# Merging the weighted sums of two graphs into one run of 128 tiled matmuls, with a separate PSUM pool for the scores and an earlier attention window

## Chip, cores, metric

One core of one Trainium2 chip. The metric is the device time of one execution in microseconds (us). "The trace" is the profiler's record of one execution.

## The reference, cut to what matters

Two layers on 128 graphs of 128 nodes with 256 features, all in fp32. Layer 0 applies graph attention twice and a feed-forward part. Layer 1 is an eight-head attention in which each of four relations has its own value projection:

```python
scores = jnp.einsum('bhid,bhjd->bhij', q, k) / np.sqrt(dh)
attn = jax.nn.softmax(scores, axis=-1)
for r in range(Wv.shape[0]):                     # 4 relations
    v_r = (src @ Wv[r] + bv[r]).reshape(Bb, Nn, h, dh).transpose(0, 2, 1, 3)
    mask = (adj_matrix == r)[:, None]
    out = out + jnp.einsum('bhij,bhjd->bhid', attn * mask, v_r)
attn_out = out.transpose(0, 2, 1, 3).reshape(Bb, Nn, Dm) @ Wo + bo
x = _ln(src + attn_out, g1, beta1)
ff = jax.nn.gelu(x @ W1 + b1, approximate=False) @ W2 + b2
return _ln(x + ff, g2, beta2)
```

## The kernel before

The 128 graphs go through in 32 groups of four (G = 4). Each stage of a group is a Python generator. A stage has a **window**, a begin and an end in units of one group, and the stages of all groups are interleaved by that clock; a scheduler then fixes the order on each engine. The parts that matter here:

```python
TB, KB = 4, 7                                    # buffers of T and of tok
ps = ctx.enter_context(tc.tile_pool(name="ps", bufs=5, space=PSUM))
# 8 PSUM banks in use: "mm" 5, "tr" 2 (transposes), "av" 1 (weighted sums)

def weights(b):                                  # scores and softmax of graph b
    scores = [ps.tile([P, DC, 2, N], F32, name="mm") for _ in range(2)]
    for c in range(DC):
        for h in range(2):                       # two halves of the array's rows
            rows = ts(h, P // 2)
            nc.tensor.matmul(scores[h][:, c], qT[rows, c, ts(b, N)], kbd[c][rows, b],
                             start=True, stop=True, tile_position=(h * P // 2, 0))
    ...                                          # maximum, 4 exponentials a bank, division

def weighted(ms, v):                             # 32 calls, 64 instructions
    po = ps.tile([P, DC, N], F32, name="av", bufs=1)
    for c in range(DC):
        for r in reversed(range(R)):
            for q in reversed(range(HC)):        # 4 column tiles of 32
                last = nc.tensor.matmul(po[ts(q, DH), c], v[:, r, ...], ms[q // 2][r][:, ...],
                                        start=r == R - 1, stop=r == 0, tile_position=(0, q * DH))
    ...

for b in range(G):
    ...
    ms = by_relation(b, es.pop(0))               # 8 masked tiles on VectorE
    v = values(b)
    yield 1.5
    with tc.high_priority(offset=200):
        oT, last = weighted(ms, v)
        if b + 2 < G:
            with tc.issue_after(last.ins):       # on TensorE's queue: not ahead of this run
                es.append(weights(b + 2))
    ...

stages = (..., (stage_attention, 16, 2.0, 3.0), ...)   # steps, begin, end
```

Every fp32 matmul call shows as two instructions in the trace (transposes as one), so one graph's scores are a block of 8 and its weighted sum is a run of 64.

## Time and profile before

| | before |
|---|---|
| median (3 runs) | 3509.6 us |
| profiled span | 3506.2 us |
| TensorE busy | 98% |
| steady period of one group | 107.33 us |
| span minus 32 periods ("start and end") | 71.6 us |

In profile lines, PE is TensorE's matmuls, PEld its weight loads, DVE VectorE, ACT ScalarE, POOL GpSimd; L352 is line 352 of the kernel. In a timeline line, the first number is the start, the second the modelled length of the merged group of instructions. I take the time of a group from the start of the next one. The period is the distance between the first query projections (L286) of two groups.

### The profile page before, as it was taken

To read this page: it belongs to the slowest core of one execution; us is meant where nothing else is said; L and a number is where in the kernel's file an instruction comes from. 1 tells how busy PE (TensorE), PEld (TensorE's weight loads), DVE (VectorE), ACT (ScalarE), POOL (GpSimd) and SP (SyncE) were. 2 spreads that over 40 slices of the span, in tenths; PEclk is the share of its full clock that TensorE was granted. 3 is DMA by queue.
4 is the path that set the end of the run, shared out by engine and by line. 5 is a ranking of instruction groups with operands and counts; after the bars stand their busy time and mean duration, and the time that the engine had idled before them with its cause. 6 is when DMAs were issued, how large, how long until landed. Compare 5 with 4: busy or idle time off the path is not lost.

```text
span 3506.2 us, 52290 instructions
## 1 busy us (share of the span) xinstructions
PE 3442.3 (98%) x20496; PEld 2256.7 (64%) x20496; DVE 1602.0 (46%) x3529; ACT 1692.8 (48%) x4702; POOL 1167.7 (33%) x1352
## 2 busy tenths in 40 slices
PE   7999999999999999999999999999999999999998
PEld 5566666666666666666666666666666666666655
DVE  2444445444445444454344554444544445544453
ACT  3455445555445554455554455544555444555342
POOL 2223323233233233332332332433323323324332
PEclk8999999999999999999999999999999999999999
DMA  4000000000000000000000000000000000000000
GB/s 179 7 10 22 22 22 16 7 22 22 22 16 13 16 22 22 22 16 7 22 22 22 16 7 22 22 22 22 16 7 22 22 22 10 7 10 7 7 7 13
DMA packets 23925, 70.87 MB, mean 20 GB/s; under 512 B 2432, under 2 KB 6016, under 8 KB 23552
## 3 DMA queue, kind: packets, MB, share of 16 engines
q1 hardware_dynamic: 23680, 67.53, 5.5%
q8 instruction: 162, 2.65, 0.3%
q14 instruction: 83, 0.68, 0.1%
HBM read 50.75 MB, written 16.78 MB: 19 GB/s over the span
## 4 chain that ended last, share of the span: by engine, by line
PE 85%; ACT 9%; DVE 5%; issue 1%; POOL 0%; DMA 0%; SPq 0%; ACTq 0%; POOLq 0%; DVEq 0%
PE mm L210 25%; PE mm L222 20%; PE mm L340 12%; PE av L352 7%; ACT kbd L295 5%; PE mm L255 3%; PE mm L286 3%; PE mm L379 3%; PE tr L327 3%; PE mm L304 2%; PE mm L273 2%; PE mm L292 2%; PE mm L264 2%; ACT e L242 2%; PE tr L193 1%; ACT tr L235 1%
## 5 line engine op out<-in xcount | busy, mean ns | idle before, releaser
L331 DVE SCALAR_TENSOR_TENSOR m<-at,tr 128x512 f32<-128x512 int32 x1024 | 628.3, 679 | 229.3 <-PE av L352 134.5
L184 POOL TENSOR_TENSOR tok<-tok,ln_rows 128x512 f32<-128x512 f32 x508 | 634.8, 1274 | 280.0 <-PE tr L193 260.8
L316 POOL TENSOR_TENSOR e<-e,s 128x512 f32<-128x512 f32 x256 | 264.0, 1041 | 759.1 <-DVE mv L170 666.2
L213 ACT ACTIVATE fT<-mm,col 128x512 f32<-128x512 f32 x512 | 337.9, 687 | 331.4 <-PE mm L210 327.4
L210 PE MATMUL mm<-T,wf 128*128 128x512 f32 x1024 | 473.7, 601 | 11.7 <-ACT T L197 11.7
L210 PE MATMUL mm<-T,w 128*128 128x512 f32 x1024 | 476.4, 604 | 3.6 <-ACT T L197 0.7
L340 PE MATMUL mm<-wv,T 128*128 128x512 f32 x1024 | 461.0, 592 | 0.6 <-ACT e L314 0.6
L222 PE MATMUL mm<-w,fT 128*128 128x256 f32 x2048 | 460.3, 381 | 0.0
L222 PE MATMUL mm<-wf,fT 128*128 128x256 f32 x2048 | 456.0, 381 | 0.0
L178 ACT ACTIVATE tok<-tok,nmr,rstd 128x256 f32<-128x256 f32 x512 | 265.8, 590 | 389.1 <-POOL nmr L176 389.1
L222 PEld LDWEIGHTS mm<-w,fT 128*128 128x128 f32 x2048 | 384.2, 190 | 69.7 <-issue 21.5
L223 DVE TENSOR_TENSOR tok<-tok,mm 128x512 f32<-128x512 f32 x128 | 88.0, 687 | 733.5 <-PE mm L222 730.5
L222 PEld LDWEIGHTS mm<-wf,fT 128*128 128x128 f32 x2048 | 384.3, 190 | 57.1 <-issue 7.4
L314 ACT ACTIVATE e<-mm,nm 128x128 f32<-128x128 f32 x1024 | 357.9, 385 | 17.1 <-DVE nm L310 16.7
L210 PEld LDWEIGHTS mm<-T,w 128*128 128x128 f32 x1024 | 182.9, 190 | 221.0 <-issue 184.9
L210 PEld LDWEIGHTS mm<-T,wf 128*128 128x128 f32 x1024 | 185.9, 191 | 212.9 <-issue 186.6
L340 PEld LDWEIGHTS mm<-wv,T 128*128 128x128 f32 x1024 | 189.5, 190 | 203.3 <-issue 197.1
L244 POOL TENSOR_TENSOR e<-e,s 128x512 f32<-128x512 f32 x64 | 66.5, 1039 | 737.1 <-DVE s L243 737.1
L352 PEld LDWEIGHTS av<-m,v 128*32 128x32 f32 x8192 | 217.3, 110 | 69.8 <-issue 59.6
L352 PE MATMUL av<-m,v 128*32 128x128 f32 x8192 | 252.0, 275 | 7.4 <-DVE v L341 4.7
L356 ACT COPY oT<-av 128x256 f32<-128x256 f32 x128 | 46.9, 366 | 394.0 <-PE av L352 394.0
L314 ACT ACTIVATION_READ_ACCUMULATOR e<-mm,nm 128x1 f32 x1024 | 231.9, 226 | 0.0
(64 smaller groups left out, 3735.6 us busy)
## 6 DMA issues: line engine op xcount, KB each, us to landing
xt<-in_xT_dram SPq DMA_DIRECT2D x32, 512.0 KB, 3.3
tok<-in_x_dram SPq DMA_DIRECT2D x32, 512.0 KB, 3.5
out_dram<-tok SPq DMA_DIRECT2D x31, 512.0 KB, 2.6
at<-in_adjT_dram SPq DMA_DIRECT2D x32, 256.0 KB, 2.7
wf<-in_wf_dram SPq DMA_DIRECT2D x2, 1024.0 KB, 10.9
w<-in_w_dram SPq DMA_DIRECT2D x2, 1024.0 KB, 12.8
ln_rows<-in_rows_dram SPq DMA_DIRECT2D x1, 1024.0 KB, 9.8
wv<-in_wv_dram SPq DMA_DIRECT2D x1, 1024.0 KB, 10.4
```

The lines of the kernel that those rows point to most:

```text
L178: nc.scalar.activation(y[:, b], y[:, b], AF.Identity, bias=nmr[:, b:b + 1], scale=rstd[:, b:b + 1])
L184: engine.tensor_tensor(y[:, b:b + 2], y[:, b:b + 2], v[:, None, :].to_broadcast([P, 2, D]), op)
L210: nc.tensor.matmul(p, win[:, c, ts(f0 + i, P)], hT[:, c], start=c == 0, stop=c == DC - 1)
L213: nc.scalar.activation(t, p, func, bias=bin_[:, f0 + i:f0 + i + 1])
L222: nc.tensor.matmul(p[:, b - b2_], fT[f][:, ts(b, N)], wout[:, f], start=f == 0, stop=f == FC - 1)
L255: nc.tensor.matmul(p, xt[:, c, ts(b, N)], wx[:, c], start=c == 0, stop=c == DC - 1)
L295: nc.scalar.activation(kbd[c][rows, :, q % 2], p[rows], AF.Identity, bias=bk[rows, c:c + 1])
L314: nc.scalar.activation(e[:, q], p[:, q], AF.Exp, bias=nm[:, q:q + 1], accum_out=s[:, q:q + 1])
L316: nc.gpsimd.tensor_mul(e, e, per_row(s, N))
L331: nc.vector.scalar_tensor_tensor(m, ab, r, pT, op0=OP.is_equal, op1=OP.mult)
L340: nc.tensor.matmul(p, hT[:, f, ts(b, N)], wv[:, f, r:r + 2], start=f == 0, stop=f == DC - 1)
L352: last = nc.tensor.matmul(po[ts(q, DH), c], v[:, r, c * P + q * DH:c * P + (q + 1) * DH], ms[q // 2][r][:, c * 2 + q % 2], start=r == R - ...
```

## The change

The intent is to visit the 32-column shape of the array half as often, and to have the next scores follow the run directly, from banks of their own. Sixteen masked tiles need space, which smaller pools and an earlier, longer attention window give back.

```diff
-    TB, KB = 4, 7
+    TB, KB = 3, 6
-    ps = ctx.enter_context(tc.tile_pool(name="ps", bufs=5, space=PSUM))
+    ps = ctx.enter_context(tc.tile_pool(name="ps", bufs=3, space=PSUM))
     ... (fT: FC + 1 to FC buffers; cap, wh, oT: 2 to 1)
-            scores = [ps.tile([P, DC, 2, N], F32, name="mm") for _ in range(2)]
+            scores = [ps.tile([P, DC, 2, N], F32, name="sc", bufs=2) for _ in range(2)]
-                    m = wk.tile([P, HC, N], F32, name="m", bufs=DC * R)
+                    m = wk.tile([P, HC, N], F32, name="m", bufs=2 * DC * R)
-        def weighted(ms, v):
-            po = ps.tile([P, DC, N], F32, name="av", bufs=1)
+        def weighted(work):
+            po = ps.tile([P, 2, DC, N], F32, name="av", bufs=1)
+            for i, (ms, v) in reversed(list(enumerate(work))):
     ... (the same 32 matmuls for each of two graphs, one copy out)
-        for b in range(G):
+        for b0 in range(0, G, 2):
     ... (masks and values of b0 and b0 + 1)
+            with tc.high_priority(offset=200):
+                oT, last = weighted(work)
+                if b0 + 2 < G:
+                    with tc.issue_after(last.ins):
+                        es.append(weights(b0 + 2))
+            yield 1.5
     ... (output projection and addition for both graphs)
+            if b0 + 2 < G:
+                es.append(weights(b0 + 3))
+            yield 1.5
-              (stage_attention, 16, 2.0, 3.0), (stage_ff1, 8.5, 3.15, 3.65))
+              (stage_attention, 16, 1.5, 2.8), (stage_ff1, 8.5, 3.15, 3.65))
```

More of the change, by code (lines that the diff above doesn't have):

```diff
@@ L99, in graph_layers @@
     MW = D + 4
-    m = wload("M", wk.tile([P, DC, MW], F32, name="m_in", tag="wh"))
-    w2T = wload("W2T", wk.tile([P, DC, D], F32, name="w2T", tag="fT", bufs=FC + 1))
+    m = wload("M", wk.tile([P, DC, MW], F32, name="m_in", tag="wh", bufs=1))
+    w2T = wload("W2T", wk.tile([P, DC, D], F32, name="w2T", tag="fT", bufs=FC))
     first_xt = ld.tile([P, DC, T], F32, name="xt")
     nc.sync.dma_start(first_xt, xT[0])
-    w1T = wload("W1T", wk.tile([P, DC, D], F32, name="w1T", tag="fT", bufs=FC + 1))
+    w1T = wload("W1T", wk.tile([P, DC, D], F32, name="w1T", tag="fT", bufs=FC))
     first_at = ld.tile([P, G, N], I32, name="at", bufs=4)
@@ L211, in feed_forward @@
             for i, p in enumerate(pair):
-                t = wk.tile([P, T], F32, name="fT", tag="fT", bufs=FC + 1)
+                t = wk.tile([P, T], F32, name="fT", tag="fT", bufs=FC)
                 nc.scalar.activation(t, p, func, bias=bin_[:, f0 + i:f0 + i + 1])
@@ L247, in gat_block @@
     def gat_block(xg, xt, at):
-        cap = wk.tile([P, G, N], F32, name="cap")
+        cap = wk.tile([P, G, N], F32, name="cap", bufs=1)
         nc.vector.tensor_scalar(cap, at, 0, 2 * BIG, op0=OP.is_gt, op1=OP.mult)
-        wh = wk.tile([P, G, MW], F32, name="wh", tag="wh")
+        wh = wk.tile([P, G, MW], F32, name="wh", tag="wh", bufs=1)
         for b in range(G):
@@ L343, in values @@
             return v
-        def weighted(ms, v):
-            po = ps.tile([P, DC, N], F32, name="av", bufs=1)
-            for c in range(DC):
-                for r in reversed(range(R)):
-                    for q in reversed(range(HC)):
-                        last = nc.tensor.matmul(po[ts(q, DH), c], v[:, r, c * P + q * DH:c * P + (q + 1) * DH],
-                                                ms[q // 2][r][:, c * 2 + q % 2],
-                                                start=r == R - 1, stop=r == 0, tile_position=(0, q * DH))
-            oT = wk.tile([P, DC, N], F32, name="oT")
+        def weighted(work):
+            po = ps.tile([P, 2, DC, N], F32, name="av", bufs=1)
+            for i, (ms, v) in reversed(list(enumerate(work))):
+                for c in range(DC):
+                    for r in reversed(range(R)):
+                        for q in reversed(range(HC)):
+                            last = nc.tensor.matmul(po[ts(q, DH), i, c],
+                                                    v[:, r, c * P + q * DH:c * P + (q + 1) * DH],
+                                                    ms[q // 2][r][:, c * 2 + q % 2],
+                                                    start=r == R - 1, stop=r == 0, tile_position=(0, q * DH))
+            oT = wk.tile([P, 2, DC, N], F32, name="oT", bufs=1)
             nc.scalar.copy(oT, po)
@@ L363, in attention @@
         yield 1
-        for b in range(G):
-            if b % 2 == 0:
-                affine(y, "02", b)
-            ms = by_relation(b, es.pop(0))
-            v = values(b)
-            yield 1.5
-            with tc.high_priority(offset=200):
-                oT, last = weighted(ms, v)
-                if b + 2 < G:
-                    with tc.issue_after(last.ins):
-                        es.append(weights(b + 2))
+        for b0 in range(0, G, 2):
+            affine(y, "02", b0)
+            work = []
+            for b in (b0, b0 + 1):
+                ms = by_relation(b, es.pop(0))
+                work.append((ms, values(b)))
+                yield 1.5
[4 more added lines that the diff above has]
+                        es.append(weights(b0 + 2))
+            yield 1.5
+            p = ps.tile([P, 2, D], F32, name="mm")
+            for i in range(2):
+                for k in range(DC):
+                    nc.tensor.matmul(p[:, i], oT[:, i, k], wo[:, k], start=k == 0, stop=k == DC - 1)
+            nc.vector.tensor_add(y[:, b0:b0 + 2], y[:, b0:b0 + 2], p)
+            if b0 + 2 < G:
+                es.append(weights(b0 + 3))
             yield 1.5
-            p = ps.tile([P, D], F32, name="mm")
-            for k in range(DC):
-                nc.tensor.matmul(p, oT[:, k], wo[:, k], start=k == 0, stop=k == DC - 1)
-            nc.vector.tensor_add(y[:, b], y[:, b], p)
         normalised(y)
```

## The prediction

> **What bounds the kernel now.** I read the first part of the page (busy time by engine), then the chain that ended last, then two steady stretches of the trace by engine, and at last the timeline of TensorE's matmuls, start by start. The first part of the page, with the chain's shares by engine below it:
>
> ```profile
> PE 3442.3 (98%) x20496; PEld 2256.7 (64%) x20496; DVE 1602.0 (46%) x3529; ACT 1692.8 (48%) x4702; POOL 1167.7 (33%) x1352
> ...
> PE 85%; ACT 9%; DVE 5%; issue 1%; POOL 0%; DMA 0%; SPq 0%; ACTq 0%; POOLq 0%; DVEq 0%
> ```
>
> TensorE (PE) is busy 98% of the span, no other engine reaches half, and the chain is 85% PE. So only what shortens or holds up PE's queue counts. Next, busy time by engine in two adjacent stretches of 107.3 us in the middle (columns: stretch, its us, then each engine's busy us and instructions):
>
> ```profile
> 1840.00:1947.30 107.30, 106.81 (x641) 70.02 (x641) 49.87 (x111) 52.95 (x148) 36.51 (x42) 1.00 0.05 18
> 1947.30:2054.60 107.30, 106.81 (x641) 70.02 (x641) 49.87 (x111) 52.94 (x148) 36.51 (x42) 1.00 0.05 18
> ```
>
> The program repeats itself to the hundredth: 107.3 us for each of the 32 groups of four graphs, or 3434 us; the remaining 72 us are start and end. PE idles 0.5 us of each period, at full clock (1.00). But busy is not streaming. In the timeline (start, modelled length, engine, line) I use the distance between starts, because the lengths overlap:
>
> ```profile
> 1852.04 5.34 PE L222 MATMUL mm<-w,fT 128*128 128x256 f32 x24
> 1857.31 1.95 PE L352 MATMUL av<-m,v 128*32 128x128 f32 x64
> 1859.19 1.99 PE L222 MATMUL mm<-w,fT 128*128 128x256 f32 x8
> 1861.03 1.46 PE L273 MATMUL mm<-wh,e 128*128 128x256 f32 x6
> 1862.41 1.14 PE L304 MATMUL mm<-kbd,T 64*128 64x256 f32 x8
> 1863.48 0.70 PE L273 MATMUL mm<-wh,e 128*128 128x256 f32 x2
> ...
> 1864.78 7.07 PE L222 MATMUL mm<-w,fT 128*128 128x256 f32 x32
> 1871.69 1.03 PE L379 MATMUL mm<-wo,oT 128*128 128x256 f32 x4
> ```
>
> The undisturbed L222 costs (1871.69 - 1864.78)/32 = 0.216 us each. The 24 ahead of the weighted sum (L352, 32-column tiles) take 5.27 us instead of 5.18, so **entering** costs 0.09 to 0.10. The 64 small matmuls take 1.88 us; single starts in the trace come in fours 0.110 us apart, so 64 need 1.76, and **leaving** costs about 0.13. The 8 L222 behind it take 1.84 instead of 1.73: another 0.11 **after leaving**. One visit to the 32-column shape therefore costs about 0.10 + 0.13 + 0.11 = **0.34 us** beyond its work, and none of it shows as idle. Over all starts in the trace the medians are 96, 138 and 107 ns, for 128 such runs. The score matmuls (L304, 64-row tiles) have the same form: 96 ns in, about 0.31 out; when they follow L352 at once, the middle pair of costs falls together and some 0.2 us is saved. That happens in 35 of the 128 runs.
>
> **What the Trainium skill says.** "TensorEngine Tiling (Array Packing)", Key Properties: changing the tiling mode, not only the tile, drains the engine. The trace agrees; the sums above are its price here. "TensorE: Matmul & The Clock Gate", Step-by-step: weight loads can be pulled ahead, matmuls stay in program order; so one matmul that waits for a PSUM bank holds all behind it. "PSUM — Partial Sum Buffer", Terms and The four PSUM rules: eight banks of 512 fp32 a partition; a starting matmul clears flags for a bank and the quadrants it writes. The new 2x2x128 output fills exactly one bank, and its groups in one quadrant follow one another, so one bank is legal. "Perfetto Trace Analysis", Tensor Engine Instruction: a matmul's reported end is computed. Hence my use of starts; the trace agrees, since reported lengths overlap the next starts.
>
> **The change, part by part.**
>
> 1. *Half as many visits.* 128 runs of 64 become 64 runs of 128. The arithmetic is the same. Saved: 64 x 0.34 = **21.8 us**, all of it in PE's queue, hence on the path.
> 2. *Scores behind the run.* Before, scores of graphs 2 and 3 were queued behind runs 0 and 1, and 35 direct successions resulted. Now only graph 2's scores are tied to a run (one a group: 32); graph 3's come later and pay in and out by themselves. Three fewer at 0.2: **+0.6 us**. Having their own PSUM pool should let the 32 succeed reliably.
> 3. *Evictions.* The weighted output is copied once as 128x512 instead of twice as 128x256 (0.37 us each), and the output projection is added once (0.69 us, by the 128x512 additions) instead of twice (0.41). Both save a little on engines at half load: **0**.
> 4. *Banks.* Before: five for "mm" (scores included), two "tr", one "av". After: three "mm", two "sc", two "tr", one "av". Scores hold two banks some 6 us, from 1838.83 to the last exponential at about 1845, four times a period: 25 of 107 us. So the rest of the program had five banks three quarters of the time and now always has three. This is the cost I must guess: **+5 us** if the order of instructions adapts, more below.
> 5. *Masked tiles.* 16 buffers for 16 tiles, as 8 for 8 before: making the next ones waits for the run to end. By line group a mask costs 0.679 us on VectorE, so a pair's take 10.9 us, in about 53 us between runs; VectorE is busy 50 of 107. Hidden: **0**.
> 6. *Fewer buffers elsewhere* (T 3, tok 6, fT 8, cap and wh 1) pay for the masks, and attention moves from 2.0-3.0 to 1.5-2.8 in group units. With these windows I count at most three T tiles and six tok tiles alive: 0. At the end, attention of the last group has more feed-forward work to run beside it, where PE now waits 0.72, 0.75, 0.84, 0.55 and 3.73 us between 3446 and 3464; I allow **-2 us**.
>
> Sum: -21.8 + 0.6 + 5 - 2 = -18 us: 3509.6 - 18 = **3492 us**, 0.5% faster. A period should fall from 107.3 to about 106.8.
>
> **Rivals.** *First, three banks become the bound.* In the timeline of all engines:
>
> ```profile
> 1839.36 1.28 ACT L242 ACT_TABLE_LOAD   x1
> ...
> 1839.89 5.42 PE L210 MATMUL mm<-T,w 128*128 128x512 f32 x12
> ...
> 1845.08 1.28 ACT L213 ACT_TABLE_LOAD   x1
> ...
> 1846.38 2.42 ACT L213 ACTIVATE fT<-mm,col 128x512 f32<-128x512 f32 x4
> ```
>
> While ScalarE does exponentials and two table loads until 1846.4, it empties no feed-forward bank; four wait for it. With three, the fourth half-pair (1.72 us of PE work, from 8 L210 in 3.44 us for two banks) must wait unless something without a bank can be put there (transposes, the weighted run). For it: pairs need two banks at once. Against it: three banks are 5.2 us of L210 work, about the length of such a burst, and L222 fills one bank for 7 us. A stall of 0.3 us at each of 128 score blocks would give +38 us, about 3530; 1 us each gives over 3600.
>
> *Second, the wait moves to the run's start:* a run can begin only when sixteen masks and both value tiles are done, where it needed eight and one. For it: VectorE has 16 masks in a row. Against it: it was waited on only for 7.4 us in all before each L352, and the program yields 1.5 units of other work ahead of the run. If PE waited 1 us at each of 64 runs, 64 us would come on top and the change would lose 1.3%.
>
> *Third, the gain is bigger:* stalls of PE in the steady state outside the switches sum to about 2 us a period, counted from starts, mostly the feed-forward behind its transposes. A better interleaving could take 0.3 of that: another -10 us.
>
> **Range and chances.** Switch savings are well measured: between 17 and 23 us. Start and end may move by 6 either way; the new stalls lie between -5 and +30 with most weight near 5. This gives 3474 to 3518 for eight in ten. Faster by 2% would need 70 us, 2.2 us a period, which is nearly all switches together (14 in and out, some 2.9 us with their aftermath): 0.02. Slower by 2% needs 2.9 us of new stalls a period (2.2 plus the 0.7 saved): possible only if the first or second rival is strong: 0.05.
>
> **What will show it.** Right: 64 L352 runs of 128 in about 3.66 us each (32 x 0.110 + 0.13), a score block directly behind half of them, a period near 106.8, PE's idle time before L210 and L340 no larger. Wrong by the first rival: PE or weight-load idle before L210, L340 or L379 put down to ScalarE's fT or VectorE's additions. Wrong by the second: idle before L352 put down to the masks or values. Wrong in my count: runs of 128 split by other matmuls, or score blocks that pay in and out more often than 96 times.

## More of the kernel before

One axis needs care: profile lines count from the first instruction; where I worked from the trace's own zero, about 11 us earlier, the text says so.

## The result

The changed kernel takes **3518.43 us** (median of 6, 3517.05 to 3520.06), the kernel before 3509.33 us (median of 6). The ratio is 1.0027, with a 95% interval of 1.0014 to 1.0040. A ratio is the mean time of one kernel's runs over that of the other's of the same rounds, so not quite the ratio of the medians. The change loses 0.3%, where 0.5% was expected to be gained; the time is just above the stated range.

The page of the changed kernel, busy time by engine and the chain's shares:

```profile
PE 3456.9 (98%) x20496; PEld 2282.6 (65%) x20496; DVE 1590.6 (45%) x3465; ACT 1675.3 (48%) x4636; POOL 1169.6 (33%) x1352
...
PE 96%; DVE 1%; ACT 1%; DMA 1%; POOL 0%; SPq 0%; issue 0%; ACTq 0%; POOLq 0%; DVEq 0%
```

TensorE is still the bound, with the same 20496 matmuls, and the chain is even more purely its own. Two periods in the middle, by engine:

```profile
1840.00:1947.00 107.00, 107.00 (x641) 70.82 (x640) 49.49 (x108) 52.46 (x147) 36.61 (x42) 1.00 0.05 18
1947.00:2054.00 107.00, 107.00 (x641) 70.82 (x640) 49.49 (x108) 52.47 (x147) 36.60 (x42) 1.00 0.05 18
```

A period is 107.00 instead of 107.33 us, and PE is busy for all of it: the idle time of before (0.5 us) is gone, and the view of waits lists nothing at all for PE in this stretch. Yet only 0.33 us a period is gained. So the loss must be inside the busy time. The timeline of the same kernel around a run shows it:

```profile
1820.67 5.34 PE L222 MATMUL mm<-wf,fT 128*128 128x256 f32 x24
1825.94 3.70 PE L353 MATMUL av<-m,v 128*32 128x128 f32 x128
1829.58 1.13 PE L304 MATMUL sc<-kbd,T 64*128 64x256 f32 x8
1830.64 2.00 PE L222 MATMUL mm<-wf,fT 128*128 128x256 f32 x8
1832.47 1.92 PE L255 MATMUL mm<-wx,xt 128*128 128x260 f32 x8
1834.32 1.13 PE L304 MATMUL sc<-kbd,T 64*128 64x256 f32 x4
1835.38 1.14 PE L255 MATMUL mm<-wx,xt 128*128 128x260 f32 x4
1836.45 1.13 PE L304 MATMUL sc<-kbd,T 64*128 64x256 f32 x4
1837.51 1.15 PE L255 MATMUL mm<-wx,xt 128*128 128x260 f32 x4
```

The merged run works as planned: 1829.58 - 1825.94 = 3.64 us, against 3.66 predicted. Graph 2's scores follow it as a whole block of eight, 1.06 us. Graph 3's scores come five microseconds later **as two blocks of four**, and each block of four also takes 1.06 us (1835.38 - 1834.32 and 1837.51 - 1836.45). In the whole block, instructions for the upper and the lower 64 rows of the array alternate and their starts come in pairs 7 ns apart; a block of four serves one half only, so nothing overlaps, and every block pays the shape change on its own.

Now every distance between starts, over 20 periods, is set against an ideal stream of 0.833 ns a column: in this trace a 512-column matmul is followed after 429 ns and a 256-column one after 215 to 216, and (429 - 215.5)/256 = 0.834. Four 32-column tiles, or the two halves of the rows, count once. The fixed rest of about 2.5 ns a matmul is the "pipeline floor". The sums of what goes beyond the ideal stream:

| us a period beyond the ideal stream | before | changed |
|---|---|---|
| in, out and after the 32-column runs | 1.41 | 0.73 |
| in, out and after the score blocks, and lost overlap | 1.51 | 2.82 |
| other stalls of PE | 1.07 | 0.10 |
| pipeline floor (under 20 ns each) | 0.88 | 0.89 |
| ideal stream | 102.47 | 102.47 |
| period | 107.33 | 107.00 |

Merging saves 0.68 us a period as predicted (21.7 us in all). The scores lose 1.31 us (42 us): over the whole trace a score block not directly behind a run is entered 129 times, where the prediction counted 96. Stalls fall by 0.97 us (31 us), which the prediction had only as a rival worth 10 us. And start and end grow from 71.6 to 91.1 us: 3515.3 - 3506.2 = 9.1, about 19.5 - 32 x 0.33.

At the start of the kernel before, the first group's normalisation is covered by the second group's feed-forward (L210):

```profile
81.26 1.04 PE L193 MATMUL tr<-ident,tok 128*128 128x128 f32 x8
82.73 10.57 PE L210 MATMUL mm<-T,wf 128*128 128x512 f32 x24 [0.43 <-ACT T L197]
...
107.85 3.60 PE L286 MATMUL mm<-T,wq 128*128 128x512 f32 x8
```

At the start of the changed kernel:

```profile
62.14 13.98 PE L222 MATMUL mm<-wf,fT 128*128 128x256 f32 x64
80.51 2.16 PE L193 MATMUL tr<-ident,tok 128*128 128x128 f32 x8 [4.40 <-ACT tok L178]
83.32 3.78 PE L286 MATMUL mm<-T,wq 128*128 128x512 f32 x4 [0.65 <-ACT T L197]
...
93.38 1.88 PE L210 MATMUL mm<-T,wf 128*128 128x512 f32 x4
```

and at its end:

```profile
3404.34 0.63 PE L327 MATMUL tr<-ident,e 128*128 128x128 f32 x4 [2.92 <-DVE m L331]
3407.85 1.12 PE L327 MATMUL tr<-ident,e 128*128 128x128 f32 x4 [2.88 <-POOL e L316]
...
3412.18 5.43 PE L353 MATMUL av<-m,v 128*32 128x128 f32 x128
```

The first attention (L193, L286) now begins right behind the first feed-forward (L222) and waits for its normalisation with nothing beside it; the second group's feed-forward (L210) comes only then. The granted clock falls too: between 60 and 300 us it is at half for 23.9 us, against 6.8 before. In the last group PE waits for masks, and the run that follows takes 5.4 us, because the clock is at half from 3405.5 to 3415.8: until then its groups of four start 0.21 us apart, afterwards 0.11. So a stretch at half the clock costs at most half its length; for the start I estimate no more than 9 of the 14 us that it grew (measured below).

### The profile page after: what moved, and what is told of

Read it like the earlier page. It is cut to its first block, busy times and chain, and to the rows that moved or that the text cites. A ratio compares the mean times of both kernels' runs of the same rounds, so it can differ in the third digit from the quotient of the medians.

```text
span 3515.3 us, 51984 instructions
## 1 busy us (share of the span) xinstructions
PE 3456.9 (98%) x20496; PEld 2282.6 (65%) x20496; DVE 1590.6 (45%) x3465; ACT 1675.3 (48%) x4636; POOL 1169.6 (33%) x1352
## 4 chain that ended last, share of the span: by engine, by line
PE 96%; DVE 1%; ACT 1%; DMA 1%; POOL 0%; SPq 0%; issue 0%; ACTq 0%; POOLq 0%; DVEq 0%
PE mm L222 25%; PE mm L210 25%; PE mm L340 12%; PE av L353 7%; PE sc L304 5%; PE mm L255 3%; PE mm L383 3%; PE mm L286 3%; PE mm L292 3%; PE tr L327 3%; PE tr L193 2%; PE mm L264 2%; PE mm L273 2%; PE tr L233 1%; DMA wf<-in_wf_dram 0%; DVE m L331 0%
## 5 line engine op out<-in xcount | busy, mean ns | idle before, releaser
L316 POOL TENSOR_TENSOR e<-e,s 128x512 f32<-128x512 f32 x256 | 266.0, 1040 | 832.6 <-DVE s L315 786.6
L213 ACT ACTIVATE fT<-mm,col 128x512 f32<-128x512 f32 x512 | 348.6, 689 | 340.6 <-PE mm L210 336.5
L210 PE MATMUL mm<-T,w 128*128 128x512 f32 x1024 | 476.6, 596 | 1.5 <-ACT fT L213 0.9
L340 PE MATMUL mm<-wv,T 128*128 128x512 f32 x1024 | 475.6, 594 | 0.0
L222 PE MATMUL mm<-wf,fT 128*128 128x256 f32 x2048 | 467.2, 381 | 0.0
L210 PE MATMUL mm<-T,wf 128*128 128x512 f32 x1024 | 466.0, 598 | 0.3 <-ACT fT L213 0.2
L222 PE MATMUL mm<-w,fT 128*128 128x256 f32 x2048 | 460.4, 381 | 0.0
L222 PEld LDWEIGHTS mm<-w,fT 128*128 128x128 f32 x2048 | 387.4, 190 | 83.1 <-issue 35.7
L222 PEld LDWEIGHTS mm<-wf,fT 128*128 128x128 f32 x2048 | 380.3, 190 | 74.0 <-issue 25.0
L314 ACT ACTIVATE e<-sc,nm 128x128 f32<-128x128 f32 x1024 | 361.0, 371 | 140.8 <-DVE nm L310 121.3
L358 ACT COPY oT<-av 128x512 f32<-128x512 f32 x64 | 37.5, 586 | 730.7 <-PE av L353 730.7
L310 DVE TENSOR_REDUCE nm<-sc 128x4 f32<-128x512 f32 x256 | 167.0, 683 | 464.4 <-PE sc L304 464.4
L210 PEld LDWEIGHTS mm<-T,wf 128*128 128x128 f32 x1024 | 190.0, 191 | 212.6 <-issue 177.2
L210 PEld LDWEIGHTS mm<-T,w 128*128 128x128 f32 x1024 | 183.8, 192 | 173.1 <-issue 150.8
L295 ACT ACTIVATE kbd<-mm,col 32x512 f32<-32x512 f32 x256 | 173.7, 678 | 255.8 <-PE mm L292 252.1
L341 DVE TENSOR_TENSOR v<-mm,bv 128x512 f32<-128x512 f32 x256 | 175.1, 684 | 158.0 <-PE mm L340 158.0
L353 PE MATMUL av<-m,v 128*32 128x128 f32 x8192 | 240.3, 276 | 1.0 <-DVE v L341 1.0
```

The source lines that it names most:

```text
L210: nc.tensor.matmul(p, win[:, c, ts(f0 + i, P)], hT[:, c], start=c == 0, stop=c == DC - 1)
L213: nc.scalar.activation(t, p, func, bias=bin_[:, f0 + i:f0 + i + 1])
L222: nc.tensor.matmul(p[:, b - b2_], fT[f][:, ts(b, N)], wout[:, f], start=f == 0, stop=f == FC - 1)
L314: nc.scalar.activation(e[:, q], p[:, q], AF.Exp, bias=nm[:, q:q + 1], accum_out=s[:, q:q + 1])
L316: nc.gpsimd.tensor_mul(e, e, per_row(s, N))
L340: nc.tensor.matmul(p, hT[:, f, ts(b, N)], wv[:, f, r:r + 2], start=f == 0, stop=f == DC - 1)
```

## The experiments

Three parts of the change can be taken apart: where the scores' banks lie, the window, and the merge. Each run below was correct. All have three rounds.

### Whole score blocks

Both banks become one tile, so a graph's scores cannot start on one of them:

```diff
-            scores = [ps.tile([P, DC, 2, N], F32, name="sc", bufs=2) for _ in range(2)]
+            both = ps.tile([P, 2, DC, 2, N], F32, name="sc", bufs=1)
+            scores = [both[:, h] for h in range(2)]
```

> The changed kernel with the two score banks as one tile of two banks, so that a graph's eight score matmuls can start only when both banks are free and are no longer split into two blocks of four. Theory (the split of one score block a period ate the gain: 0.86 us for four matmuls that no longer overlap their other half, 0.41 us for one more visit to the 64-row shape): period from 107.0 to about 105.7 us, total about 3478 us, no block of four left in the steady state. Rival (the wait for both banks only moves: PE idles before the scores or behind them): period 106.6 or more, total 3505 or more.

Measured: **3482.94 us**, ratio to the kernel before 0.9926 (0.9912 to 0.9941). Period 105.60 us. The timeline at the same place of the period:

```profile
1809.43 3.70 PE L354 MATMUL av<-m,v 128*32 128x128 f32 x128
1813.06 1.13 PE L305 MATMUL sc<-kbd,T 64*128 64x256 f32 x8
1814.13 1.99 PE L222 MATMUL mm<-wf,fT 128*128 128x256 f32 x8
...
1820.10 1.13 PE L305 MATMUL sc<-kbd,T 64*128 64x256 f32 x8
1821.17 0.32 PE L233 MATMUL tr<-ident,wh 128*128 128x128 f32 x1
```

Graph 3's scores are whole (1.07 us) and come two to three microseconds later after the run than their first half did; nothing waits for that. The scores' overhead is back at 1.51 us a period, and the stalls are at 0. The split was what ate the gain. The total fell by less than 32 x 1.41 = 45 us, because start and end grew once more, to 102.5 us.

### The window alone

The kernel before, with one line changed:

```diff
-              (stage_attention, 16, 2.0, 3.0), (stage_ff1, 8.5, 3.15, 3.65))
+              (stage_attention, 16, 1.5, 2.8), (stage_ff1, 8.5, 3.15, 3.65))
```

> The kernel before with only the attention window moved to 1.5-2.8. Theory (the window makes both the dearer start and end and the vanished stalls; and score blocks get split in the shared pool too, 61 halves by the order of instructions): start and end outside 32 periods from 72 to about 90 us, stalls of PE outside shape switches from 1.07 to about 0.1 us a period, shape costs up by about 1 us a period; total about 3530 us. Rival A (stalls fell because runs were merged and pools split): stalls stay at 1.07, total about 3560. Rival B (start and end grew because of the merged runs, not of the window): start and end stay at 72, total about 3510.

Measured: 3525.31 us, ratio 1.0048 (1.0031 to 1.0064). Period 107.37, start and end 87.4 us. Stalls in the steady state fall to 0, the scores' overhead rises to 2.71 us (one block a period is split in the shared pool too, here one of the first two graphs), the runs' stays near 1.31. So the window is what removed the stalls, and what made start and end dearer: 15.8 of the 19.5 us. Both points of the theory hold.

### The changed kernel with the old window

```diff
-    TB, KB = 3, 6
+    TB, KB = 4, 6
-              (stage_attention, 16, 1.5, 2.8), (stage_ff1, 8.5, 3.15, 3.65))
+              (stage_attention, 16, 2.0, 3.0), (stage_ff1, 8.5, 3.15, 3.65))
```

> The changed kernel with the attention window back at 2.0-3.0 and four T buffers (tok stays at 6, for space). Theory (window governs start, end and stalls, the pool of two banks governs the split): start and end back to about 72 us, stalls back to about 1 us a period, still one split score block a period; period about 107.9, total about 3528. Rival (stalls fell by the merge): stalls near 0.1, period 107.0, total about 3498.

Measured: **3646.05 us**, ratio 1.039 (1.0375 to 1.0406). Period 111.73, start and end 66.8 us. Start and end went as expected, and the split stayed. But the stalls came back much larger than in the kernel before (5.0 us a period against 1.07; 54.6 us at half the clock between 500 and 3000 us add to them), so the theory missed something that the next run shows without the merge.

### Own pool for the scores, alone

The kernel before with `name="sc", bufs=2` for the scores and three mm banks.

> The kernel before with only the scores moved to their own pool of two banks and mm cut from five to three. By the order of instructions every score block but two stays whole and 64 instead of 35 follow a weighted sum directly, which is worth about 3 us. Theory (three mm banks are harmless, as no wait for banks shows in the changed kernel): total 3505 to 3512. Rival (three banks hold up PE, hidden in the changed kernel by the other window): new idle time before the feed-forward put down to ScalarE, total 3530 or more.

Measured: **3700.86 us**, ratio 1.0548 (1.0532 to 1.0563). Period 113.8 us. The rival won clearly. The view of waits, PE's first two rows (total us, times, longest):

```profile
PE mm L264 <- ACT wh L265: 61.5, 29, 2.1
PE mm L222 <- DVE tok L223: 40.2, 29, 1.4
```

Once a group, L264 (the first graph attention, one mm bank for each of four graphs) waits for L265, the ScalarE copy that empties such a bank. Around 1812, ScalarE has just done eight exponentials and four normalisations, and only then, at 1814.28, do the copies begin:

```profile
1814.28 0.95 ACT L265 COPY wh<-mm 128x258 f32<-128x258 f32 x3
1814.72 1.23 PE L264 MATMUL mm<-wh,e 128*128 128x258 f32 x2 [2.12 <-ACT wh L265]
```

In the kernel before, with five banks, this wait is not in the trace; with three the outputs wait for ScalarE's queue. Around those waits the clock drops as well: between 500 and 3000 us the trace has 22 stretches, 102 us in all, at half the clock, and none in the kernel before. By the same estimate as above that is at most 2.3 of the 6.5 us that a period lost.

### Own pool and new window, without the merge

Both edits of the last two experiments but with runs of 64.

> The kernel before with the scores in their own two banks, three mm banks, and the attention window at 1.5-2.8, but runs of 64 as before (so the changed kernel without the merge). By the order of instructions nearly no score block is split. Theory (the window keeps the graph-attention matmuls L264 away from the exponentials, so that three banks suffice; the split comes from the merge, which brings the scores of graphs 2 and 3 some 5 us apart into a pool of two banks): period about 106.5, no L264 wait for ScalarE as in the two runs with the old window, start and end about 88 us, total about 3496. Rival (three banks cost some 5 us a period in any window, and only the merge avoids it): period 110 or more, total above 3600.

Measured: 3538.75 us, ratio 1.0087 (1.0070 to 1.0103). Period 107.84, start and end 84.9 us. Nearly no block is split, as expected, so with the pool of two banks the split comes with the merge. But the wait at L264 did not vanish, against my theory; it became smaller, 1.7 us a period counted from starts, and the clock stays up here:

```profile
PE mm L264 <- ACT wh L265: 42.0, 29, 1.5
```

The period of 107.84 is about 1.3 us above what I expected, and neither that nor the rival's 110 was met.

### Scores back in the shared pool

The changed kernel with the scores in "mm" and five banks.

> The changed kernel with the scores back in the shared pool of five mm banks. By the order of instructions its shape visits and halves cost 94 us in all, against 111 in the changed kernel and 72 in the one with whole score blocks. Theory (a bank shortage is not what costs the changed kernel time; the order of the scores is): period about 106.5, total about 3500. Rival (the pools themselves cost, three banks being too few in the new window too): period below 105.8, total below 3480.

Measured: 3502.00 us, ratio 0.9980 (0.9965 to 0.9995), period 106.67 (the mean of periods of about 106.2 and 107.4), start and end 87.1 us. This agrees with the theory to 0.2 us a period: with the new window, which pool the scores come from matters through the order and splits that result, not through a shortage of banks. That holds for merged runs; without the merge three banks still cost the wait at L264 shown above. Of the 1.07 us a period over whole blocks, 0.7 are shape visits and splits, and 0.37 stalls.

### The merge alone

The kernel before with runs of 128 and sixteen masks: shared pool of five banks, old window, four T buffers and six tok. It keeps the changed kernel's smaller buffers for fT, cap, wh and oT, as all runs of 128 here do, so no run tells these from the merge.

> The kernel before with runs of 128 and sixteen masks alone: shared pool of five banks, old window 2.0-3.0 (four T buffers, six tok). By the order of instructions 58 score blocks of four appear (shape visits and halves together cost 105 us, against 92 before). Theory (merging by itself halves the visits to the 32-column shape, worth about 0.6 us a period, but brings the scores of graphs 2 and 3 close together, whose split costs over 1 us): average period 107.6 to 108.2, total about 3520. Rival (merging is worth its 21 us when the pool is left at five banks, as predicted): total about 3488.

Measured: **3676.46 us**, ratio 1.0475 (1.0456 to 1.0494), period 112.62 us. Both expectations missed. The first row of PE's waits, then the timeline of one period:

```profile
PE av L353 <- DVE m L331: 85.4, 32, 5.7
```

```profile
1813.87 0.60 PE L327 MATMUL tr<-ident,e 128*128 128x128 f32 x4
1817.04 5.37 PE L353 MATMUL av<-m,v 128*32 128x128 f32 x128 [2.57 <-DVE m L331]
...
1862.56 3.70 PE L353 MATMUL av<-m,v 128*32 128x128 f32 x128
```

One of the two runs of a group waits 2.6 us for its last mask, and then takes 5.3 us instead of 3.6, with the clock at half for 3.4 us from 1817.7. The prediction's second rival is real, but in the steady state only here, with the old window and the shared pool.

### Whole blocks with the old window

> Whole score blocks and merged runs, but the old window 2.0-3.0 (four T buffers). Theory (with three mm banks, the old window lets the four L264 outputs and the feed-forward pairs wait for ScalarE behind the exponentials): as in the changed kernel with the old window but without the split, period about 110.5, start and end about 67 us, total about 3605. Rival (the split caused those waits, by keeping ScalarE busy at the wrong time): period about 106.6, total about 3480.

The edit is that of the first experiment and that of the old window together. Measured: 3664.91 us, ratio 1.0445 (1.0429 to 1.0462), period 112.15 us, so the theory's direction was right and its size 1.6 us a period too small. The waits are the ones the prediction's first rival named, banks that ScalarE has not emptied:

```profile
PE mm L210 <- ACT fT L213: 63.6, 59, 2.4
PE mm L341 <- ACT fT L213: 47.9, 31, 1.6
```

Here the clock stays full throughout the steady state, so these waits, with what they add around the scores, cost over 6 us a period (112.15 against 105.60 with the new window).

### A start of its own for the first group

Whole score blocks, and one exception among the windows:

```diff
+            if g == 0 and n == 3:                # attention of the first group
+                begin, end = 1.8, 2.9
```

> Whole score blocks, and the attention of the first group alone moved to 1.8-2.9, so that it no longer begins before the second group's feed-forward. Theory (20 us of the dearer start come from the first attention having nothing beside it at 80 to 90 us and at 150 to 170 us): loss at the start from 75 to 55-60 us, period unchanged at 105.6, total about 3466. Rival (the start is dearer because of the pools or the sixteen masks, not the order): total within 5 us of 3483.

Measured: **3458.78 us**, ratio 0.9856 (0.9839 to 0.9872): the fastest of all. The period is unchanged at 105.60. For the loss at the start I take the time to the ninth group's query projection less the ideal stream done by then at the steady rate: 54.5 us before, 68.4 changed, 74.7 with whole blocks, 49.3 here. These times count from the trace's own zero, so each is some 11 us too large for the span's axis (and the sum at the end, below, as much too small); their differences hold. The gain of 25 us over whole blocks is more than the 15 to 20 expected; it includes the clock, which here is never at half between 60 and 300 us, against 23.9 us with whole blocks. The start in this kernel:

```profile
63.96 13.98 PE L222 MATMUL mm<-wf,fT 128*128 128x256 f32 x64
77.77 1.04 PE L193 MATMUL tr<-ident,tok 128*128 128x128 f32 x8
79.25 10.57 PE L210 MATMUL mm<-T,wf 128*128 128x512 f32 x24 [0.43 <-ACT T L197]
...
91.44 1.98 PE L286 MATMUL mm<-T,wq 128*128 128x512 f32 x4 [0.76 <-ACT T L197]
```

The second group's feed-forward (L210) fills the time in which the first group's normalisation runs, and the attention (L286) follows.

### Start and end together

```diff
+            if g == 0 and n == 3:
+                begin, end = 2.0, 3.0
+            if g == NG - 1 and n == 3:
+                begin, end = 1.8, 3.0
+            if g == NG - 2 and n == 4:           # last but one feed-forward of layer 1
+                begin, end = 2.95, 3.9
```

> Whole score blocks; the first group's attention at 2.0-3.0 as in the kernel before, the last group's at 1.8-3.0, and the last but one feed-forward of layer 1 spread from 2.95 to 3.9 to fill the last attention. Theory (start and end are costs of the window alone): start back to about 55, end from 26 to 15 us, total about 3452, the fastest of all. Rival (sixteen masks in a row make the last and first weighted sums late whatever stands beside them): total above 3470.

Measured: 3462.54 us, ratio 0.9869 (0.9854 to 0.9884). The loss at the start is 55.1 us, as expected, but the same sum at the end is 24.9 us, hardly less than the 26.0 with whole blocks. The total meets neither the theory's 3452 us nor the rival's 3470. The edit for the end failed; the trace still shows PE waiting 4.0 us for a mask ahead of a run and 5.4 us for the last normalisation. How to fill the end stays open.

### All combinations

Steady period in us, and start and end (profiled span less 32 periods) behind it:

| banks of the scores | runs | old window | new window |
|---|---|---|---|
| shared, five mm | 64 | 107.33, 71.6 (before) | 107.37, 87.4 |
| shared, five mm | 128 | 112.62, 71.1 | 106.67, 87.1 |
| own two, three mm | 64 | 113.85, 55.9 | 107.84, 84.9 |
| own two, three mm | 128 | 111.73, 66.8 | 107.00, 91.1 (the change) |
| own, whole block, three mm | 128 | 112.15, 74.6 | 105.60, 102.5 |

In the old window the merge alone or the pool alone costs 5.3 or 6.5 us a period; in the new one each moves it by less than 1 us, and whole blocks gain 1.4. What start and end lose comes with the new window in every row.

## Why the prediction was wrong

1. *Half as many visits, 21.8 us.* Right: 0.68 us a period, 21.7 us.
2. *Scores behind the run, +0.6 us.* **This step failed.** 32 direct successions came as counted, but I took graph 3's scores to be a whole block of eight, paying in and out once. The pool hands out banks one at a time, so one block a period became two of four. The term measured +1.31 us a period, 42 us. The run with whole blocks shows that this was the cause. The prediction did list "score blocks that pay in and out more often than 96 times" as a way to be wrong; it did not see that a half block takes as long as a whole one.
3. *Evictions, 0.* Nothing in the runs contradicts it, and the output in one bank gave correct results; PE has no wait for them in the steady state.
4. *Banks, +5 us.* Wrong as a step of its own. In the changed kernel the view of waits shows none for a bank in the steady state (starts show 0.10 us a period at L264), but three banks alone cost 6.5 us a period with the old window (107.33 to 113.85). The first rival was real; the new window hides it, without the merge only in part. I treated banks and window as independent terms of a sum, which they are not.
5. *Masks, 0.* Right in the changed kernel's steady state; with the old window and the shared pool the merged run waits 2.6 us for them. What hid that wait in the changed kernel (its window, its pool) I had not used as a reason.
6. *Window, -2 us at the end.* **This step failed too.** The window removed 0.97 us of stalls a period (31 us), which I had only as a third rival worth 10 (its "about 2 us" of stalls a period were 1.07 and the pipeline floor of 0.88), and start and end cost 19.5 us, of which I had the sign wrong. The run with the window alone shows both, with 15.8 of the 19.5 us, and the run with a later first attention shows the mechanism at the start. The end was not settled: its waits for masks are in the trace, but my remedy did not move them.

Together: -21.7 (visits) + 42 (scores) - 31 (stalls) + 19.5 (start and end) = +9 us, the measured difference of the spans. Two errors of opposite sign brought the time close to the predicted range, so its nearness was no merit of the reasoning.

## What to carry to other kernels

A change of the array's shape costs TensorE time that no view shows as idle; count it from the starts of matmuls. Where two matmuls overlap because they use different halves of the array, allocate their outputs as one tile, or a scheduler that gets banks one at a time may pull them apart. When a change bundles a window, a pool and a merge, measure each alone and in pairs: here each part alone was slower, two of the three by over 4%, and the start and end must be read apart from the steady period.

## What the Trainium skill lacked or had wrong

- "TensorEngine Tiling (Array Packing)", Key Properties, says that a mode switch drains the engine, without a price. Here: 96 ns in, about 140 ns out and 107 ns in the matmul after, 0.34 us for a visit to the 32-column shape; some 0.4 us for a visit to the 64-row shape.
- "TensorE: Matmul & The Clock Gate", HAM oscillation, gives as its abstract rule that idle gaps over about 3.4 us re-throttle the clock. Here the clock halved for 3.4 to 6.8 us in most periods when the longest single gap of the steady state was 2.1 us (scores in their own pool, old window), 2.3 us (the changed kernel with the old window) or 2.6 us (merge alone). It did not at 1.5 us (own pool, new window) or 1.6 us (whole blocks, old window). The page's next section does say that frequent short idles can do it too, but gives no length.
